# A four-layer attention and feed-forward kernel: turned rows by VectorE and transfers, slot stores on GpSimd's queue, biases inside the opening's products

## The chip, the cores and the metric

The kernel runs on one core of one Trainium2 chip. A core has five engines that run side by side: TensorE (PE, matrix products), VectorE (DVE), ScalarE (ACT), GpSimd (POOL) and SyncE (SP, which here only issues transfers). Each engine works through its own queue of instructions in the order in which they were written, and waits for others by semaphores. Transfers (DMAs) can be issued from SP, ACT and POOL. The metric is the time of one execution on the device in microseconds (us).

## The reference

The computation carries x of shape (4, 256, 256) through four layers; every layer adds an attention over a context of shape (4, 512, 128) and then a feed-forward block. All of it is in float32.

```python
x = x + _L0_xattn_ref(_layernorm(x, axis=-1), ctx_1024, ...)   # 16 heads of 16, head norms, biases
x = x + _L0_ffn_ref(_layernorm(x, axis=-1), ...)               # best 4 of 64 rank-16 maps
x = x + _L1_xattn_ref(_layernorm(x, axis=-1), ctx_1024, ...)   # 16 heads of 128, 8 key heads
x = x + _L1_ffn_ref(_layernorm(x, axis=-1), ...)               # shared expert + best 2 of 8 experts
x = x + _L2_xattn_ref(...); x = x + _L2_ffn_ref(...)           # one of 2 experts per token
x = x + _L3_xattn_ref(...); x = x + _L3_ffn_ref(...)           # best 64 tokens of each batch
```

Layer 0 projects the normalised rows to queries (with bias bq) and the context to keys and values (with biases; the last 16 context tokens have weights and biases of their own), takes the mean out of each head and divides by its deviation, and then attends. Layer 1's block sends every token to two of eight experts.

## The kernel before, in words

The four engines that compute are put under an order written out by hand (`manual_schedule`, line 1033 and later): their instructions stand in their queues as the Python code issues them. SP's queue alone is ordered by the compiler's scheduler, by what is ready.

The matrix products are float32, and the profile shows two records for each. A product needs its operands with the contracted dimension on the partitions, so rows have to be turned. Normalised rows are turned by `layernorm_T` (line 938): four TensorE transposes against an identity into a PSUM bank, then one ScalarE copy to SBUF (line 947). `context_T` (line 906) does the same for the 512 tokens of one batch's context. `turned1` (line 2189) does it for the rows that the first routed block needs, and stores these rows to DRAM (`xd`).

The opening (lines 1037 to 1572). Loads are issued from SP and ACT, among them the rows of norm parameters `prm` (line 1048, from ACT) and three short bias rows `crow` (lines 1061 to 1065, from SP). VectorE takes head means out of the weights and of `crow`. `spread_biases` (line 1165) multiplies `takes`, a small 0/1 matrix, with `crow`, so that every partition holds the biases; ScalarE copies that to `bqk`. `project_q` and `project_k` (lines 1184 and 1200) make the products, and a VectorE addition puts `bqk` to them on the way out of PSUM. The class `Scale` squares, sums, and scales the heads; `transposed` (line 1337) turns them; the first `scores` follow. `warm` (line 1441) issues products that nobody reads, to fill gaps on TensorE.

Attention of layers 1 to 3 (line 1795): 32 units (4 batches of 8 pairs of heads). Every unit makes the next unit's queries, four score products, the exponentials, and four value products. In unit 3 of a batch, the next batch's rows are normalised (`tokens`, line 2039); in unit 5 `layernorm_T` turns them (line 2046); in unit 6 `x_sums` (line 2048, VectorE) reads them, and in unit 7 the first queries of the next batch. In layer 1, `beside1` (line 2248) does the same for the routed block's rows: normalised in unit 4, turned in unit 5, read in unit 6 by `chosen`.

The routed block of layer 1 (lines 2265 to 2622). 20 blocks of 128 slots each belong to one expert. For block j the methods are `gather` (line 2436, an indirect DMA from POOL that brings 128 rows of `xd` into `xg`, four buffers), `turn_in` (two TensorE transposes of `xg`), `rise`, `fall`, `last_rows` (products) and `store` (line 2497: ScalarE scales the result into `yr`, SP's queue writes it to DRAM, `yd`). The loop that orders them is:

```python
for j in range(-1, NBLK + 1):                    # line 2567
    if j + 2 < NBLK:
        if j + 2 >= 4:
            blocks[j + 2].gather()
        if j >= 0:
            blocks[j + 2].weights()
        blocks[j + 2].turn_in()
    ...                                          # rise of j+1, fall of j
        if j % 2 or j == NBLK - 1:               # every second turn: last_rows, then store, of both
```

So blocks go by pairs. In the turn after a pair's stores, the code issues the gather of the block four further on than the pair's first, and TensorE's first work of that turn is to transpose what this gather brings. When all 20 are stored, `Back` (line 2505) gathers the results from `yd`, and the weights of layer 2 are folded (`folding`, line 981; its products `pn` go to the banks "o" and "s").

The routed block of layer 2 ends with a loop over its last blocks (line 3046), in which `backs[n].add()` and the norm of the next layer's first rows stand at i = 6, and `tokens` at i = 7.

Of the kernel before, what the change touches and what calls it, by code (L numbers as in the profile page):

```python
# [17 lines left out]
P = 128  # L18
# [818 lines left out]
def bounded_path(ctx: ExitStack, tc: tile.TileContext, t, out: bass.AP, over):  # L837
# [10 lines left out]
    w0 = first.enter_context(tc.tile_pool(name="w0", bufs=2, side="right"))  # L848
    ring = first.enter_context(ExitStack())
# [104 lines left out]
    def normalised(name):  # L954

        after = layernorm(0, f"{name}_0")
        for b in range(B):
            _, xnT = after
            if b + 1 < B:
                after = layernorm(b + 1, f"{name}_{b + 1}")  # L960
            yield b, xnT
# [19 lines left out]
    def folding(L, m_sb, n_sb):  # L981

        for i in range(4):
            h0 = 4 * i
            if (L, i) not in raws:
                load_raw(L, i)
            wq_t, wk_t, wv_t, wo_t = raws.pop((L, i))
            for g in range(2):
                pm = bank("mm", [P, ND, 2, DC], f"pm_{L}_{i}_{g}")
                for d in range(ND):  # L990
                    for h in range(2):
                        nc.tensor.matmul(  # L992
                            pm[:, d, h, :],
                            lhsT=wq_t[:, 2 * g + h, d * P : (d + 1) * P],
                            rhs=wk_t[:, g, :],
                            start=True,
                            stop=True,
                        )
                h1 = h0 + 2 * g
                nc.scalar.mul(m_sb[:, :, h1 : h1 + 2, :], pm, 1.0 / math.sqrt(P))  # L1000
                m2 = rawp.tile([P, ND, 2, DC], F32, tag="m2", name=f"m2_{L}_{i}_{g}", bufs=1)
                for h in range(2):
                    nc.scalar.activation(
                        m2[:, :, h, :], m_sb[:, :, h1 + h, :], AF.Square,
                        accum_out=msq[:, L - 1, h1 + h : h1 + h + 1],
                    )
                pn = bank("mm" if "ring" in banks else "os"[g], [P, 2, D], f"pn_{L}_{i}_{g}")
                nc.tensor.matmul(  # L1008
                    pn, lhsT=wv_t[:, g, :], rhs=wo_t[:, 2 * g : 2 * g + 2, :], start=True, stop=True
                )  # L1010
                nc.vector.tensor_copy(n_sb[:, h1 : h1 + 2, :], pn)
                yield
# [20 lines left out]
    with tc.manual_schedule(engines={E.PE, E.Activation, E.DVE, E.Pool}):  # L1033
# [13 lines left out]
        for i, n in enumerate(("qn", "kn", "knd")):  # L1047
            nc.scalar.dma_start(prm[:, i], t[f"L0_{n}"].partition_broadcast(P))
# [6 lines left out]
        rows1 = w0.tile([3, D + 3 * P], F32, tag="oT0", name="rows1")  # L1055
# [3 lines left out]

        brow = l0.tile([1, 2, 2 * D], F32, tag="brow", name="brow")  # L1060
# [31 lines left out]
        make_identity(nc, ident)  # L1092
        nc.gpsimd.memset(neghalf, -0.5)

# [3 lines left out]
        nc.gpsimd.memset(takes, 1.0)  # L1098
        for i, base, cm, p in (
            (0, 0, -1, 0), (1, -1, 1, 0), (1, 1, -1, 0), (2, RD - 1 - P, P, -1), (2, 2 * P - RD, -P, 1),  # L1100
        ):
            nc.gpsimd.affine_select(
                out=takes[:, i, :], in_=takes[:, i, :], compare_op=ALU.is_ge, fill=0.0, base=base,
                pattern=[[p, P]], channel_multiplier=cm,
            )
# [78 lines left out]
        def project_q(b):  # L1184
            raw_heads(b)
            pq = bank("mm", [P, NC, D], f"pq0_{b}")
            for c in range(NC):
                for d in range(ND):
                    nc.tensor.matmul(
                        pq[:, c, :],  # L1190
                        lhsT=xnTs[b][:, d, c * P : (c + 1) * P],
                        rhs=wq0[:, d, :],
                        start=(d == 0),
                        stop=(d == ND - 1),
                    )
            return lambda: nc.vector.tensor_tensor(
                qks[b][:, :NC, :], pq, bqk[:, 0:1, :].to_broadcast([P, NC, D]), ALU.add
            )

        def project_k(b, k0):  # L1200
            raw_heads(b)
            pk = bank("mm", [P, 2, D], f"pk{b}_{k0}")
            for k in (k0, k0 + 1):
                last = k == NK - 1
                ck = c_last[:, b % 2, 0, :] if last else cT[:, b, k * P : (k + 1) * P]
                nc.tensor.matmul(pk[:, k - k0, :], lhsT=ck, rhs=wk0[:, 0, :], start=True, stop=not last)
                if last:
                    nc.tensor.matmul(
                        pk[:, k - k0, :], lhsT=c_last[:, b % 2, 1, :], rhs=wk0[:, 1, :], start=False, stop=True
                    )  # L1210
            bias = bqk[:, 1:3, :] if k0 + 2 == NK else bqk[:, 1:2, :].to_broadcast([P, 2, D])
            return lambda: nc.vector.tensor_tensor(qks[b][:, NC + k0 : NC + k0 + 2, :], pk, bias, ALU.add)
# [20 lines left out]
        class Scale:  # L1233


            def __init__(self, b):
                self.src = by_head(qks[b])
                self.dst = pad.rearrange("p c q (h x) -> p c (q h) x", x=HD0)
                self.sq = w0.tile([P, NQK, H0, HD0], F32, tag="hs", name=f"hs{b}", bufs=1)
                self.v, self.r, self.e = (  # L1240
                    small.tile([P, NQK, H0], F32, tag=f"h{i}", name=f"h{i}_{b}", bufs=2) for i in "vre"
                )

            def square(self, on_act, a=0, z=NQK):
                sq, src = self.sq[:, a:z], self.src[:, a:z]
                if on_act:
                    nc.scalar.activation(sq, src, AF.Square)
                else:
                    nc.gpsimd.tensor_tensor(sq, src, src, ALU.mult)
# [25 lines left out]
            def scaled(self, a=0, z=NQK):  # L1275
                nc.vector.tensor_tensor(
                    self.dst[:, a:z], self.src[:, a:z],
                    self.r[:, a:z, :, None].to_broadcast([P, z - a, H0, HD0]), ALU.mult,
                )
# [57 lines left out]
        def transposed(b, c0, wait=False):  # L1337
# [5 lines left out]
            pt = bank("t", [P, 2, 2, P], f"pT{b}_{c0}")  # L1343
# [176 lines left out]
        norm = Norm(0, "a0_0")  # L1520
        last_context(0)
# [5 lines left out]
        centred(by_head(crow), by_head(crow), head_sums(by_head(crow), 3), 3)  # L1527
        wk = by_head(wkv, 2 * HD0)[:, :, :, :HD0]
        centred(by_head(wk0), wk, head_sums(wk))
        for n in range(2):  # L1530
            wv = by_head(wkv, 2 * HD0)[:, n, :, HD0:].rearrange("p (q j o) x -> p o q j x", q=2, o=2)
            for o in range(2):
                nc.gpsimd.tensor_copy(wvo[:, n, o].rearrange("p (q j) x -> p q j x", q=2), wv[:, o])
        columns_of_norms()
        warm(3)
        add_q = project_q(0)
        spread_biases()
        add_q()
        sc0 = Scale(0)
        sc0.square(True, 0, NC)  # L1540
        add_k = [project_k(0, k0) for k0 in range(0, NK, 2)]
        add_k[0]()
        sc0.square(True, NC, NC + 2)
        sc0.sum(0, NC)
        add_k[1]()
        sc0.power(0, NC)
        sc0.square(True, NC + 2, NQK)
        context_T(1)
        sc0.sum(NC, NC + 2)
        ones_of_values()  # L1550
        sc0.root_aside(0, NC)
        last_context(1)
        sc0.sum(NC + 2, NQK)
        sc0.power(NC, NQK)
        kept = []
# [3 lines left out]
        warm(2)  # L1559
        sc0.scaled(0, NC)  # L1560
        second = transposed(0, 0, True)
        warm(4)
        sc0.root(NC, NQK)
        sc0.scaled(NC, NC + 2)
        transposed(0, 2)
        sc0.scaled(NC + 2, NQK)
        second()
        transposed(0, 4)
        warm(2)
# [19 lines left out]
        def between(b, i):  # L1589

            n = b + 1
            if n == 1:
                if i == 0:
                    for k0 in range(0, NK, 2):
# [16 lines left out]
            elif n < B:  # L1611
                if i == 0:
                    context_T(n)
# [17 lines left out]
            if n + 1 < B:  # L1631
                if i == (5 if n == 1 else 6):
# [162 lines left out]
    def attention(L, m_sb, n_sb, first_xnT=None, after=None, at_end=None, chunk=None, within=None):  # L1795
# [13 lines left out]
        with tc.tile_pool(name=f"att{L}", bufs=2) as ap:  # L1809
            xnTs, xns, xxs, norms, qTs, pqs, outs, sums = {}, {}, {}, {}, {}, {}, {}, {}  # L1810
# [223 lines left out]
            for n, (b, hp) in enumerate(units):  # L2034
                if b + 1 < B:
                    if hp == 1:
                        norms[b + 1] = Norm(b + 1, f"a{L}_{b + 1}")
                    elif hp == 3:
                        xns[b + 1] = norms[b + 1].tokens()
# [5 lines left out]
                if b + 1 < B and hp == 5:  # L2045
                    xnTs[b + 1] = layernorm_T(xns[b + 1], f"a{L}_{b + 1}")
# [142 lines left out]
    def turned1(b, xn):  # L2189
        nc.sync.dma_start(xd[b * S : (b + 1) * S, :].rearrange("(c p) d -> p c d", p=P), xn)  # L2190
        xnT1[b] = fx.tile([P, ND, S], F32, tag=f"xnT{b}", name=f"xnT_f1_{b}")
        pt = bank("t", [P, ND, S], f"pxn_f1_{b}")
# [55 lines left out]
    def beside1(b, hp):  # L2248
        if b == 0:
            load_waiting(2)  # L2250
        if b > 0:
            if hp == 3:
                ahead1[b] = Norm(b - 1, f"f1_{b - 1}")
            elif hp == 4:
                ahead1[b] = ahead1[b].tokens()
            elif hp == 5:
                turned1(b - 1, ahead1[b])
# [7 lines left out]
    with tc.manual_schedule(engines={E.PE, E.Activation, E.DVE, E.Pool}):  # L2265
        back = ExitStack()
        backp = back.enter_context(tc.tile_pool(name="back", bufs=4, side="right"))
        with tc.tile_pool(name="f1", bufs=2) as fp:
# [161 lines left out]
            class Block:  # L2430
# [66 lines left out]
                def store(self):  # L2497
# [5 lines left out]
                    nc.sync.dma_start(yd[j * P : (j + 1) * P, :], yr)  # L2503
# [483 lines left out]
    with tc.manual_schedule(engines={E.PE, E.Activation, E.DVE, E.Pool}):  # L2987
# [3 lines left out]
        with tc.tile_pool(name="f2", bufs=2) as fp, tc.tile_pool(name="raw3", bufs=4) as rawp:  # L2991
# [54 lines left out]
            for i in range(5, NBLK2):  # L3046
# [5 lines left out]
                if i + 1 < NBLK2:  # L3052
                    rise2(i + 1)
                    if i + 2 < NBLK2:
                        blocks2[i + 2].weights(fp)
                    blocks2[i + 1].either()
# [7 lines left out]
                if i == 6:  # L3064
                    for n in range(NC):
                        backs[n].add()
                    norm = Norm(0, "a3_0")
                if i == 7:
# [385 lines left out]
```

## Time and profile before

| what | value |
|---|---|
| time, median of 3 runs | 1388.01 us (1386.84 to 1388.09) |
| the profiled execution | 1386.64 us, of which the span from the first to the last instruction is 1384.9 us |
| TensorE busy | 1374.5 us (99%) |
| VectorE busy | 887.1 us (64%) |
| GpSimd busy | 683.9 us (49%) |
| ScalarE busy | 580.2 us (42%) |
| DMA packets | 50849, of them 2544 from GpSimd's queue |
| first scores of layer 0 start at | 21.28 us |
| the 20 routed blocks of layer 1 | about 581.5 to 634 us |

A row of the timeline gives the start in us, the length in us of what is merged in it, the engine, the line, the operation, and in brackets how long the engine sat idle before it and what ended that. A row of the windows gives a stretch's borders and length, then the busy time (and count) of PE, PEld (weight loads), DVE, ACT and POOL, then the granted clock of TensorE, the busy share of the DMA engines and GB/s.

### The profile page before, as it was taken

The page shows a single profiled execution, that of the slowest core. Times are in us where ns is not written, and L with a number is a line of the kernel's source. Part 1 is how long each engine was busy: PE and PEld are TensorE (multiplying, and loading weights), DVE is VectorE, ACT ScalarE, POOL GpSimd, SP SyncE. Part 2 cuts the span into 40 slices and gives each one's busy share as a digit, 9 for nine tenths or more (in the row PEclk, how much of TensorE's full clock was granted, in tenths as well). Part 3 has the DMA queues.
Part 4 walks back from the last instruction along what each step waited for, and adds up shares of the span by engine and source line. Part 5 has one row for each costly group of instructions (what it writes and reads, how often), then busy time and mean ns, then how long its engine had stood idle before and what let it go on. Part 6 is the DMA issues. An engine that isn't in the chain of part 4 may idle for free.

```text
span 1384.9 us, 20011 instructions
## 1 busy us (share of the span) xinstructions
PE 1374.5 (99%) x7277; PEld 908.1 (66%) x7277; DVE 887.1 (64%) x2026; ACT 580.2 (42%) x1148; POOL 683.9 (49%) x829
## 2 busy tenths in 40 slices
PE   9999999999999999999999999999999999999998
PEld 7665676566656667887565666666975656666667
DVE  6667863665666547655666756558656758566676
ACT  5766454433343332356434333333364344333331
POOL 4223333566565445232577654556315675445561
PEclk9999999999999999999999999999999999999999
DMA  5000220300000001172110000000332000000001
GB/s 170 2 1 2 76 77 21 78 17 1 9 0 9 1 9 34 47 238 67 39 54 8 16 1 9 0 0 16 120 117 65 8 4 4 0 1 0 1 0 34
DMA packets 50849, 47.10 MB, mean 34 GB/s; under 512 B 8755, under 2 KB 46868, under 8 KB 50742
## 3 DMA queue, kind: packets, MB, share of 16 engines
q1 hardware_dynamic: 46406, 37.69, 8.9%
q0 software_dynamic: 2544, 6.95, 1.8%
q8 instruction: 60, 0.98, 0.3%
q10 hardware_dynamic: 1792, 1.10, 0.3%
q14 instruction: 47, 0.39, 0.1%
HBM read 38.78 MB, written 6.95 MB: 33 GB/s over the span
## 4 chain that ended last, share of the span: by engine, by line
PE 95%; POOL 2%; DVE 1%; DMA 1%; issue 0%; ACT 0%; ACTq 0%; SPq 0%; POOLq 0%; DVEq 0%
PE ps L1923 23%; PE po L1931 23%; PE paq L1893 6%; PE pao L1893 5%; PE pbq L1893 4%; PE pbo L1893 4%; PE ps L1378 3%; PE po L1388 2%; PE pyf L1512 2%; PE paf L1462 2%; PE pgu L2471 2%; PE psh L2292 2%; PE py L2017 2%; PE pn L1008 1%; PE pb L2876 1%; PE pm L992 1%
## 5 line engine op out<-in xcount | busy, mean ns | idle before, releaser
L1942 POOL TENSOR_TENSOR half<-pT 128x1024 f32<-128x1024 f32 x93 | 218.4, 2349 | 287.1 <-ACT pT L1926 214.8
L1923 PE MATMUL ps<-qT,cT 128*128 128x512 f32 x768 | 345.6, 593 | 0.0
L1931 PE MATMUL po<-pT,c_sb 128*128 128x512 f32 x768 | 345.3, 592 | 0.0
L1926 ACT ACTIVATE pT<-ps,mbias 128x512 f32<-128x512 f32 x384 | 263.8, 687 | 155.3 <-PE ps L1923 140.0
L1931 PEld LDWEIGHTS po<-pT,c_sb 128*128 128x128 f32 x768 | 145.8, 190 | 183.2 <-issue 183.2
L1923 PEld LDWEIGHTS ps<-qT,cT 128*128 128x128 f32 x768 | 138.9, 190 | 138.4 <-issue 136.3
L1935 ACT COPY oT<-po 128x512 f32<-128x512 f32 x96 | 56.2, 586 | 265.2 <-PE po L1931 265.2
L1978 POOL TENSOR_TENSOR oT<-oT,wide 128x512 f32<-128x512 f32 x84 | 106.8, 1292 | 0.0
L1903 DVE TENSOR_TENSOR qT<-qT,paq 128x128 f32<-128x128 f32 x90 | 25.5, 283 | 96.0 <-ACT qT L1902 96.0
L1382 ACT ACTIVATE pT<-ps 128x512 f32<-128x512 f32 x128 | 66.0, 602 | 25.8 <-PE ps L1378 25.6
L1950 DVE TENSOR_TENSOR half<-half 128x512 f32<-128x512 f32 x96 | 71.8, 748 | 2.7 <-POOL half L1940 2.5
L1952 DVE STREAM_TRANSPOSE turned<-half 128x512 f32<-128x512 f32 x96 | 68.3, 711 | 6.3
L1903 DVE TENSOR_TENSOR w<-w,pao 128x128 f32<-128x128 f32 x21 | 6.0, 286 | 103.0 <-ACT w L1902 103.0
L1893 PE MATMUL paq<-xnT_a,m_sb 128*128 128x128 f32 x360 | 71.4, 280 | 0.0
L1893 PE MATMUL paq<-xx,m_x 128*128 128x128 f32 x360 | 69.6, 275 | 0.0
L1893 PEld LDWEIGHTS paq<-xnT_a,m_sb 128*128 128x128 f32 x360 | 57.2, 192 | 16.7 <-issue 8.5
L1956 DVE TENSOR_REDUCE sums<-turned 128x16 f32<-128x512 f32 x96 | 65.9, 686 | 3.3
L1893 PE MATMUL pao<-n_x,ox 128*128 128x128 f32 x336 | 65.0, 275 | 0.0
L1902 ACT COPY qT<-paq 128x128 f32<-128x128 f32 x90 | 23.9, 265 | 94.1 <-PE paq L1893 94.1
L1906 DVE TENSOR_TENSOR qT<-qT,pbq 128x384 f32<-128x384 f32 x90 | 49.9, 554 | 9.7 <-DVE qT L1905 0.5
L1893 PEld LDWEIGHTS paq<-xx,m_x 128*128 128x128 f32 x360 | 54.7, 192 | 0.0
L1977 DVE STREAM_TRANSPOSE wide<-rz 128x512 f32<-128x512 f32 x84 | 54.4, 686 | 0.0
(490 smaller groups left out, 2547.3 us busy)
## 6 DMA issues: line engine op xcount, KB each, us to landing
wq<-in_L_wqT SPq DMA_DIRECT2D x11, 512.0 KB, 4.2
wo<-in_L_wo SPq DMA_DIRECT2D x11, 512.0 KB, 5.1
yd<-yr SPq DMA_DIRECT2D x20, 128.0 KB, 3.6
xd<-xn_f SPq DMA_DIRECT2D x8, 256.0 KB, 2.3
w<-in_F_w SPq DMA_DIRECT2D x4, 512.0 KB, 3.3
wk<-in_L_wkT SPq DMA_DIRECT2D x11, 128.0 KB, 4.0
wv<-in_L_wvT SPq DMA_DIRECT2D x11, 128.0 KB, 4.4
yd<-yb SPq DMA_DIRECT2D x9, 128.0 KB, 2.4
```

The lines of the kernel that those rows point to most:

```text
L1382: nc.scalar.activation(pT[kp][:, j], ps[j], AF.Exp)
L1893: nc.tensor.matmul(p[:, at, :], lhsT=lhsT, rhs=rhs, start=(k == 0 and at == 0), stop=(k == len(of) - 1 and i == which[-1]),)
L1923: nc.tensor.matmul(ps, lhsT=cT[:, b, k * P : (k + 1) * P], rhs=qT, start=True, stop=True)
L1926: nc.scalar.activation(pT[:, k, :], ps, AF.Exp, bias=mbias[:, b, k : k + 1])
L1931: nc.tensor.matmul(po, lhsT=c_sb[:, b, k, :], rhs=pT[:, k], start=(k == 0), stop=(k == NK - 1))
L1935: done["head"] = nc.scalar.copy(raw, po).ins
L1942: nc.gpsimd.tensor_tensor(half, pT[:, 0:2], pT[:, 2:4], ALU.add)
L1950: nc.vector.tensor_tensor(part, half[:, 0], half[:, 1], ALU.add)
L1952: nc.vector.transpose(turned.rearrange("p f i -> p (f i)"), part)
L1956: nc.vector.tensor_reduce(sums[b, hp // 4][:, hp % 4, :], turned, AX.X, ALU.add)
L1977: nc.vector.transpose(wide, rzs[b, hp // 4][:, hp % 4, :, None].to_broadcast([P, NB, 32]))
L1978: eng.tensor_tensor(outs[b, hp], outs[b, hp], wide.rearrange("p f i -> p (f i)"), ALU.mult)
```

## The change

- `layernorm_aside` turns rows without TensorE: two VectorE transposes, each of 32x32 squares within 128x256, and then 16 DMAs of SP's queue, each moving one 32-partition group of squares (4 runs of 32 floats per partition) to its place. It replaces `layernorm_T` in the attention of layers 1 to 3 (issued in unit 3 with the tokens; 3 batches of each layer) and the turning in `turned1` for the first three batches (issued in unit 4). `turned_aside` does the same for the contexts of batches 2 and 3 in layer 0, two and more units before they are read, in place of `context_T`. Rows of layer 0, and the rows at the beginnings of layers, are still turned by TensorE.
- The store of a slot block is issued from `nc.gpsimd` in place of `nc.sync`.
- In the opening the loads of `prm` move from ACT's queue to POOL's. `crow` and `takes` get 128 rows (the unused ones zero, `crow` cleared by GpSimd first), and for batch 0 each of the six 128x256 pieces of q and k gets one further product `takes` x `crow` accumulated into its PSUM bank; `Scale` then reads PSUM directly. The VectorE additions of batch 0 and the early `spread_biases` go; `spread_biases` is issued in the first turn of batch 0's attention, for the later batches. `takes` is built after the first norm. In SP's queue the three loads of `crow` now stand behind the loads of all contexts and all rows of x. Some fillers are added, some removed.
- The folding of layer 2 uses bank "s" (four buffers) for `pn`. In the last loop of layer 2's routed block the `add`s move to i = 7, before `either`, the norm to the end of i = 7, the tokens to i = 8.

```diff
+    def turned_aside(dst, src, name):
+        y = squares([P, 4, 4, 32], f"y_{name}", True)
+        nc.vector.transpose(
+            y.rearrange("p q n s -> p n q s"), src.rearrange("p (n q s) -> p n q s", q=4, s=32)
+        )
+        to = dst.rearrange("p (n i s) -> p i n s", i=4, s=32)
+        for i in range(4):
+            for q in range(4):
+                nc.sync.dma_start(to[32 * q : 32 * q + 32, i], y[32 * i : 32 * i + 32, q])
+
+    def layernorm_aside(xn, name, xnT, soon=False):
+        y = squares([P, 4, ND, NC, 32], f"y_{name}", soon)
+        for c in range(NC):
+            nc.vector.transpose(
+                y[:, :, :, c].rearrange("p q d s -> p d q s"), xn[:, c, :].rearrange("p (d q s) -> p d q s", d=ND, s=32)
+            )
+        to = xnT.rearrange("p d (c i s) -> p i d c s", c=NC, s=32)
+        for i in range(4):
+            for q in range(4):
+                nc.sync.dma_start(to[32 * q : 32 * q + 32, i], y[32 * i : 32 * i + 32, q])
+        return xnT
...
-                pn = bank("mm" if "ring" in banks else "os"[g], [P, 2, D], f"pn_{L}_{i}_{g}")
+                pn = bank("mm" if "ring" in banks else "s" if L == 2 else "os"[g], [P, 2, D], f"pn_{L}_{i}_{g}")
...
-            nc.scalar.dma_start(prm[:, i], t[f"L0_{n}"].partition_broadcast(P))
...
-        rows1 = w0.tile([3, D + 3 * P], F32, tag="oT0", name="rows1")
+        rows1 = w0.tile([P, D + 3 * P], F32, tag="oT0", name="rows1")
...
+        nc.gpsimd.memset(crow, 0.0)
...
+            nc.gpsimd.dma_start(prm[:, i], t[f"L0_{n}"].partition_broadcast(P))
...
+                if b == 0:
+                    nc.tensor.matmul(pq[:, c, :], lhsT=takes[:, 0, :], rhs=crow[:, 0, :], start=False, stop=True)
+            if b == 0:
+                return pq
...
+                if b == 0:
+                    nc.tensor.matmul(
+                        pk[:, k - k0, :], lhsT=takes[:, 1 + int(last), :], rhs=crow[:, 0, :], start=False, stop=True
+                    )
+            if b == 0:
+                return pk
...
-        spread_biases()
-        add_q()
...
+        pieces = {0: project_q(0)}
+        for k0 in range(0, NK, 2):
+            pieces[NC + k0] = project_k(0, k0)
+        sc0 = Scale(0, pieces)
...
                 if i == 0:
+                    spread_biases()
                     for k0 in range(0, NK, 2):
                         project_k(n, k0)()
...
-                    context_T(n)
...
+                if i == 2:
+                    turned_aside(cT[:, n + 1, :], c_sb[:, n + 1].rearrange("p k c -> p (k c)"), f"c{n + 1}")
...
                     elif hp == 3:
-                        xns[b + 1] = norms[b + 1].tokens()
+                        name = f"a{L}_{b + 1}"
+                        xnTs[b + 1] = layernorm_aside(norms[b + 1].tokens(), name, rows_tile(name))
...
-                if b + 1 < B and hp == 5:
-                    xnTs[b + 1] = layernorm_T(xns[b + 1], f"a{L}_{b + 1}")
...
             elif hp == 4:
-                ahead1[b] = ahead1[b].tokens()
-            elif hp == 5:
-                turned1(b - 1, ahead1[b])
+                turned1(b - 1, ahead1[b].tokens(), True)
...
-                    nc.sync.dma_start(yd[j * P : (j + 1) * P, :], yr)
+                    nc.gpsimd.dma_start(yd[j * P : (j + 1) * P, :], yr)
...
+                    else:
+                        for n in range(NC):
+                            backs[n].add()
...
-                if i == 6:
-                    for n in range(NC):
-                        backs[n].add()
+                if i == 7:
                     norm = Norm(0, "a3_0")
-                if i == 7:
+                if i == 8:
                     xn = norm.tokens()
```

## The prediction

> **What bounds the kernel now.** I read the page's busy times and chain first, then the waits of TensorE, then windows by stage, then the timelines of the two stages that the change reorders.
>
> ```profile
> PE 1374.5 (99%) x7277; PEld 908.1 (66%) x7277; DVE 887.1 (64%) x2026; ACT 580.2 (42%) x1148; POOL 683.9 (49%) x829
> PE 95%; POOL 2%; DVE 1%; DMA 1%; issue 0%; ACT 0%; ACTq 0%; SPq 0%; POOLq 0%; DVEq 0%
> ...
> PE pyb L2902 <- DVE yb L2906: 1.2, 1, 1.2
> PE pn L1008 <- DVE n_sb L1011: 0.3, 1, 0.3
> ```
>
> TensorE is never free: its waits add up to some 6 us, of which 1.2 and 0.3 are places that the change touches. So a transpose taken from TensorE is a gain of its full time, and a stall put before TensorE is a loss of its full time. Only the opening (scores start at 21.28) is a chain through all engines.
>
> In the routed blocks TensorE is dense too. The rows of one pair of blocks, engine by engine (timelines; the last from the DMA list, with the median us from issue to landing):
>
> ```profile
> 580.42 0.95 POOL L2438 DMA_INDIRECT xg<-xd,who  x1 [1.41 <-PE pxg L2446]
> ...
> 587.22 0.38 PE L2495 MATMUL pyr<-wd,gR 48*128 x1
> 587.53 0.44 PE L2446 MATMUL pxg<-ident,xg 128*128 128x128 f32 x2
> 592.28 0.44 PE L2446 MATMUL pxg<-ident,xg 128*128 128x128 f32 x2
> ...
> 587.63 0.84 ACT L2500 ACTIVATE yr<-pyr,wslot 128x256 f32<-128x256 f32 x2 [0.46 <-PE pyr L2495]
> 588.13 1.04 SPq L2503 DMA_DIRECT2D yd<-yr  x2
> ...
> 578.07 0.95 POOL L2438 DMA_INDIRECT xg<-xd,who  x1 [0.30 <-issue]
> 638.06 0.94 POOL L2512 DMA_INDIRECT yg<-yd,where  x1 [23.16 <-DMA yd<-yr]
> ...
> xg<-xd,who POOLq DMA_INDIRECT x25, 3.2
> ```
>
> A pair takes 587.53 to 592.28, 4.75 us. Block 4's gather was issued at 580.42, as soon as its buffer was free, 7.1 us before TensorE turned its rows (587.53). This lead exists because POOL's queue holds nothing but gathers here.
>
> **Part 1, the slots' stores on POOL's queue.** The loop issues the two stores of a pair, and in the next turn the gather for that turn's `turn_in`. In the built order of the changed kernel POOL's queue reads: gathers 0 to 3, stores 0 and 1, gathers 4 and 5, stores 2 and 3, gathers 6 and 7, and so on; and TensorE's first instruction after `last_rows` of blocks 0 and 1 is the transpose of block 4, with a wait for its gather. So the gather is now queued behind stores that wait for ScalarE, which waits for TensorE's last rows: a loop through four engines, once for each pair. With the end of `last_rows` (587.60) as zero:
>
> - ScalarE's first `yr` is ready and the first store can issue at 0.55 (SP's row: 588.13).
> - Two stores on POOL. No row shows a plain store there. Lower bound: the 0.34 of SP's issue plus the 0.30 gap, 0.65 each. Nearest row: an indirect DMA of equally many rows on the same queue, 0.95 + 0.30 = 1.25. I take 1.25; upper bound 2.
> - The gather issues at 0.55 + 2.5 = 3.05 and lands 3.2 later (the row; 2.7 to 3.7 in this stage), at 6.25; TensorE goes on at about 6.35 in place of -0.07: a stall of 6.4 us.
>
> The second gather follows 1.25 after the first, and TensorE needs it 2.05 later (587.53 to 589.57), so it costs nothing. Stalls come before blocks 4, 6, ... 18: eight, 8 x 6.4 = 51.2 us. Nothing else can run on TensorE meanwhile, since it too works in order.
>
> Then the clock. The granted clock (the third figure from the right of a window's row) reads 1.00 from the start, so by this column a restarted TensorE is at full speed, and the sum stays 51.2. But the fillers at the start were slow:
>
> ```profile
> 1.52 4.21 PE L1445 MATMUL pwarm<-ident 128*128 128x128 f32 x18 [1.52 <-POOL ident masks.py:199]
> 5.53 1.06 PE L910 MATMUL pcT<-ident,c_sb 128*128 128x128 f32 x4
> ...
> 18.65 1.06 PE L1445 MATMUL pwarm<-ident 128*128 128x128 f32 x8
> 19.68 1.23 PE L1346 MATMUL pT<-ident,pad 128*128 128x128 f32 x8
> ...
> 2.00:4.00 2.00, 2.00 (x11) 2.00 (x11) 0.27 (x2) 0.00 (x0) 2.00 (x9) 1.00 0.62 202
> ```
>
> 18 records in 4.01 us are 223 ns each, later 8 in 1.03 are 129. [...] No stall of this length is in the trace, so the fall is not shown; I take it, as the start shows the slow state: 8 x 8.6 = 68.8 us. Loads of layer 2's weights, tied to the stores' ScalarE copies, move with the blocks.
>
> **Part 2, turning without TensorE.** Removed: nine `layernorm_T` in attention, three in `turned1`, two `context_T`; each 4 transposes, 0.44 us from start to start (587.53's two cost 0.22 to 0.27; `pxn` at 1020.00 to 1020.43 is 0.43). 14 x 0.44 = -6.2 us, and as many ScalarE copies of 0.59 that nobody waited for. Added: two VectorE transposes, by the 128x512 row of 0.71 some 0.76 the two; VectorE is busy 64% and in unit 3 needs its sums a unit (8.43 us) later: nothing. 16 DMAs on SP, at 0.35 to 0.58 an issue (rows of line 894) 7 us, the last landing 2 to 4 later: some 11 us. Cover: tokens in unit 3, `x_sums` in unit 6, 25 us; for `turned1` end of unit 4 to end of unit 6, 17 us; the contexts 15 us. SP's loads that wait for the head of unit 2 stand among them, but that is over by then. If a batch were late it would hold VectorE at `x_sums` and then the queries; I leave 0 to +5 for it.
>
> **Part 3, the opening.** What the biases now wait for:
>
> ```profile
> 4.93 0.52 SPq L1063 DMA_DIRECT2D rows<-in_L_bdca  x1
> 7.93 0.41 DVE L1152 TENSOR_REDUCE hm<-rows 3x16 f32<-3x256 f32 x1 [0.27 <-DMA rows<-in_L_bdca]
> ...
> 21.28 1.25 PE L1378 MATMUL ps<-qT,kT 32*128 32x256 f32 x16
> ```
>
> The last bias load issued at 4.93 and landed 3.0 later. In the new order it is SP's thirteenth load, behind x of batch 3, and each of SP's loads waits for an earlier landing; that x waits for the second half of `wkv`, which landed at 7.1 (SP's next load, held for it, went out at 7.11) and now shares the engines with two more contexts and rows (to 7.9). Three issues of 0.4 to 0.65 later the last bias load goes out at about 9.4 and lands at 12.3. VectorE's two steps (0.41 each): 13.15. First bias product 13.2; TensorE's queue is stuck behind it, with the q and k products of 0.45 each: q ready at 15.0 (in place of 13.5), k at 16.8 and 19.05. Then square 0.63, sum 0.86, scaling of q 0.68, the root 0.7, scaling of k 0.65, transposes 0.45, columns 0.8: scores at about 24.1, +2.8 us. If the biases were early, the three additions saved would make it 20.8 (-0.5); if TensorE fell cold in its 3 us wait, +5.5. `prm` on POOL holds the first `rstd` by up to 0.7, inside this wait. `spread_biases` moves into dense attention: three products, +1.4.
>
> **Small ones.** Fold bank -0.3; the adds behind `z` free line 2902's wait, -1.2.
>
> **Sum** on the profiled execution: 1386.6 + 68.8 - 6.2 + 2.8 + 1.4 - 1.5 = 1451.9; its median run is 1.4 above it, so 1453 us.
>
> **The rivals.**
> - The stalls come, the clock stays: 1453 - 8 x 2.2 = 1435. For it: the column of 1.00. Against: the fillers.
> [...]
> - The other side: stores do not hold the gathers, because POOL passes over a waiting DMA. Then 1388.0 - 6.2 + 2.8 + 1.4 - 1.5 = 1384.5, just faster. It decides where a gather goes out before the pair's stores have. Against: the row at 638.06 sat 23 us on one wait, and the queues of SP and ACT stood behind waiting loads in the opening. From a stall of 0.4 us on (3.5 / 8) the change is slower.
> [...]
>
> **How the numbers follow.** Full stalls with the fall of the clock 0.60 (1440 to 1470); stalls with a full clock 0.18; short stalls 0.13; heavier 0.05; no stalls 0.04. The range leaves out the last two and the ends of the others: 1422 to 1472. Slower by over 0.2% (2.8 us, about what a measurement of this kernel can tell) 0.96, faster 0.03, same 0.01.
>
> **What would show it.** Right: the stretch of the routed blocks grows from 52 to some 120 us; TensorE sits idle eight times before `pxg`, 6 us each, released by the DMA of `xg`; POOL's rows alternate two stores and two gathers, stores waiting for `yr`; records of `pgu` after a stall near twice their length; no `pxn` in units 5; no wait of VectorE for turned rows; first scores near 24. Wrong: gathers that still run 7 us ahead, or stalls of another length (then the POOL row of a store and the gather's landing say which term).

## The result, and the profile after

The changed kernel takes 1461.39 us (median of 5 runs, 1460.76 to 1462.91) against 1387.64 for the kernel before (5 runs): a ratio of 1.0534, 95% interval 1.0519 to 1.0549, so 5.3% slower. 1453 was predicted, in a range of 1422 to 1472. The place and the kind of the loss were as forecast. The length of the opening and the landing times of the gathers were not, and two small costs came up that the sum did not have.

The page of the changed kernel, its busy times, the chain of work that ended last, and two of its costliest groups (busy us, mean ns of one, idle time before it and what ended that):

```profile
PE 1390.6 (95%) x7241; PEld 922.3 (63%) x7241; DVE 896.7 (61%) x2049; ACT 573.6 (39%) x1134; POOL 699.2 (48%) x853
...
PE 89%; issue 5%; POOL 3%; DMA 1%; DVE 1%; ACT 0%; SPq 0%; POOLq 0%; DVEq 0%
...
L2486 PE MATMUL pxg<-ident,xg 128*128 128x128 f32 x40 | 10.9, 366 | 54.0 <-DMA xg<-xd,who 54.0
...
L2543 POOL DMA_DIRECT2D yd<-yr x20 | 11.5, 578 | 96.0 <-ACT yr L2540 96.0
```

TensorE was at 99% of the span and is at 95%. Its busy time rose by 16 us although 56 transposes left it: the same products take longer. The list of its waits (engine, line, what it waited for; total, times, longest) has two that are new:

```profile
PE pxg L2486 <- DMA xg<-xd,who: 54.0, 8, 8.4
PE pq L1222 <- DVE rows L1181: 5.6, 1, 5.6
```

The wait of `pyb` for `yb` (1.2) and that of `pn` (0.3) are gone, and none for turned rows has come. The routed blocks, all engines (timeline):

```profile
594.79 0.84 ACT L2540 ACTIVATE yr<-pyr,wslot 128x256 f32<-128x256 f32 x2 [0.45 <-PE pyr L2535]
595.57 1.17 POOL L2543 DMA_DIRECT2D yd<-yr  x2 [11.54 <-ACT yr L2540]
595.66 0.37 SPq L998 DMA_DIRECT2D n_sb<-in_L_wqT  x1
...
597.04 1.01 POOL L2478 DMA_INDIRECT xg<-xd,who  x1 [0.30 <-issue]
597.16 0.51 SPq L998 DMA_DIRECT2D n_sb<-in_L_wo  x1
...
603.09 0.66 PE L2486 MATMUL pxg<-ident,xg 128*128 128x128 f32 x2 [8.33 <-DMA xg<-xd,who]
603.54 2.77 PE L2511 MATMUL pgu<-xgT,we 128*128 128x128 f32 x12
607.38 2.09 PE L2511 MATMUL pgu<-xgT,we 128*128 128x128 f32 x12
...
611.35 1.15 POOL L2543 DMA_DIRECT2D yd<-yr  x2 [12.01 <-ACT yr L2540]
612.80 1.00 POOL L2478 DMA_INDIRECT xg<-xd,who  x1 [0.30 <-issue]
```

This is the forecast loop: `last_rows`, `yr`, two stores, and only then the gather for which TensorE stands still. The eight stalls are 8.33, 5.10, 8.42, 5.12, 8.34, 5.12, 8.30 and 5.26 us. The long ones are those at which SP sends out layer 2's weights (595.66 to 597.67). After a stall the 12 records of `pgu` take 2.77 us, and those of the next block up to 2.15; undisturbed they take 1.49. The windows of the opening and of the stage's first half (length; busy us, with records, of PE, PEld, DVE, ACT and POOL; granted clock, DMA share, GB/s) in the changed kernel:

```profile
0.00:21.00 21.00, 13.37 (x63) 11.49 (x64) 8.40 (x24) 3.77 (x7) 8.81 (x29) 0.84 0.70 199
...
578.00:640.00 62.00, 38.00 (x200) 32.49 (x200) 16.31 (x48) 12.77 (x38) 14.58 (x18) 0.78 0.24 78
```

The same stretches in the kernel before:

```profile
0.00:21.00 21.00, 18.67 (x103) 16.50 (x104) 14.74 (x38) 8.97 (x19) 11.35 (x48) 1.00 0.63 191
...
578.00:640.00 62.00, 61.79 (x433) 51.33 (x433) 29.36 (x79) 31.64 (x95) 17.84 (x19) 1.00 0.55 168
```

In the blocks TensorE now works 38 of 62 us, at a mean granted clock of 0.78, where it worked 61.8 at 1.00. The opening is at 0.84 in place of 1.00. So the column does show falls of the clock, which it had not shown in the kernel before. The opening in rows, and two windows of it:

```profile
11.32 0.57 SPq L1085 DMA_DIRECT2D rows<-in_L_bdca  x1
...
14.01 0.41 DVE L1176 TENSOR_REDUCE hm<-rows 3x16 f32<-3x256 f32 x1 [3.63 <-DMA rows<-in_L_bdca]
...
14.96 1.19 PE L1222 MATMUL pq<-rows 128*128 128x256 f32 x2 [5.57 <-DVE rows L1181]
...
18.52 0.60 ACT L1287 ACTIVATE hs<-pq 128x512 f32<-128x512 f32 x1 [10.31 <-PE pq L1222]
...
24.81 1.50 PE L1385 MATMUL pT<-ident 128*128 128x128 f32 x12
...
29.32 1.15 PE L1420 MATMUL ps<-qT,kT 32*128 32x256 f32 x16
...
14.00:16.00 2.00, 1.04 (x3) 0.89 (x4) 1.67 (x7) 0.00 (x0) 0.00 (x0) 0.50 0.26 69
16.00:18.00 2.00, 2.00 (x6) 1.63 (x5) 0.00 (x0) 0.00 (x0) 0.00 (x0) 0.50 0.40 80
```

The bias rows land at 14.0, the first products after TensorE's wait run at a granted clock of 0.50, q is ready at 18.5, and the first scores start at 29.32 in place of 21.28: +8.0.

Booked by places that both profiled executions have (start of the record, before and after):

| place | before | after | shift | since the last |
|---|---|---|---|---|
| first scores of the first layer | 21.3 | 29.3 | +8.0 | opening +8.0 |
| first scores of the second layer | 224.3 | 232.2 | +7.9 | +0.9 behind the first scores (the size is that of the run of the opening alone, below), two contexts -0.9 |
| lists of the routed stage, `plist` | 568.4 | 573.9 | +5.5 | six turnings, -2.4 |
| transposes of block 0 | 579.8 | 586.9 | +7.1 | +1.6: not in the prediction |
| last `pxg` of the blocks | 623.4 | 701.3 | +77.9 | stalls and clock, +70.8 |
| lists of the two-expert stage | 958.3 | 1035.2 | +76.9 | three turnings, -1.0 |
| last `pyb` of that stage | 1018.0 | 1093.6 | +75.6 | order of the adds, -1.3 |
| last `pxg` of the last stage | 1368.5 | 1442.7 | +74.2 | three turnings, -1.4 |
| end of the span | 1384.9 | 1461.2 | +76.3 | +2.1: not in the prediction |

### The profile page after: what moved, and what is told of

Read it like the earlier page. It is cut to its first block, busy times and chain, and to the rows that moved or that the text cites. A ratio compares the mean times of both kernels' runs of the same rounds, so it can differ in the third digit from the quotient of the medians.

```text
span 1461.2 us, 20280 instructions
## 1 busy us (share of the span) xinstructions
PE 1390.6 (95%) x7241; PEld 922.3 (63%) x7241; DVE 896.7 (61%) x2049; ACT 573.6 (39%) x1134; POOL 699.2 (48%) x853
## 4 chain that ended last, share of the span: by engine, by line
PE 89%; issue 5%; POOL 3%; DMA 1%; DVE 1%; ACT 0%; SPq 0%; POOLq 0%; DVEq 0%
PE ps L1963 22%; PE po L1971 22%; PE paq L1933 6%; PE pao L1933 5%; PE pbq L1933 4%; PE pbo L1933 4%; PE ps L1420 3%; PE po L1430 2%; PE pyf L1554 2%; PE paf L1504 2%; PE psh L2332 1%; PE py L2057 1%; PE pm L1014 1%; PE pn L1030 1%; PE pb L2916 1%
## 5 line engine op out<-in xcount | busy, mean ns | idle before, releaser
L1933 PEld LDWEIGHTS paq<-xnT_a,m_sb 128*128 128x128 f32 x360 | 57.5, 192 | 18.2 <-issue 9.2
L2522 DVE TENSOR_TENSOR gT<-sg,pgu 128x128 f32<-128x128 f32 x20 | 5.8, 288 | 92.3 <-ACT sg L2517 92.3
L2486 PE MATMUL pxg<-ident,xg 128*128 128x128 f32 x40 | 10.9, 366 | 54.0 <-DMA xg<-xd,who 54.0
L2543 POOL DMA_DIRECT2D yd<-yr x20 | 11.5, 578 | 96.0 <-ACT yr L2540 96.0
```

Source lines behind the costliest of these rows:

```text
L1933: nc.tensor.matmul(p[:, at, :], lhsT=lhsT, rhs=rhs, start=(k == 0 and at == 0), stop=(k == len(of) - 1 and i == which[-1]),)
```

## The experiments

None of these kernels leaves a part of the computation out. Each ratio is against the kernel before as it ran on the same chip at the same time (1387.8 or 1388.7 us there), so the ratio is the safer number; a plain difference from 1461.4 us can be off by about 1 us.

**The parts alone.** First the changed kernel with its one line of the store undone:

```diff
-                    nc.gpsimd.dma_start(yd[j * P : (j + 1) * P, :], yr)
+                    nc.sync.dma_start(yd[j * P : (j + 1) * P, :], yr)
```

> The changed kernel with one line undone: the slots' stores on SP again. Theory (the gathers queue behind the stores): the eight stalls of 54.0 us go, and with them the 16 us that the products after them lose to the clock; what is left beside the kernel before is the opening (scores 8.0 us later), the products of spread_biases (+1.4), the turning (-6.2) and the small edits (-1.5): 1387.6 + 1.7 = 1389, and a stretch of routed blocks of 52 us. Rival (the rest of the change takes part in the loss, as by its small transfers): over 1400.

Measured: 1389.74 us (12 runs), ratio 1.0013 (1.0004 to 1.0021). Of the 74 us, 72 hang on this line; what is left of the change is 2 us of loss. The opposite, that line alone in the kernel before:

> The kernel before with that one line changed: the slots' stores on GpSimd and nothing else. Theory: all of the 54.0 us of stalls and 16 us of clock: 1387.6 + 70 = 1458, granted clock near 0.78 in the routed blocks. Rival A (the stalls come, the clock falls for another reason, as the colder opening): 1387.6 + 54 = 1442. Rival B (the stores do not hold the gathers): 1387 to 1389.

Measured: 1459.94 us (4 runs), ratio 1.0520 (1.0502 to 1.0539). Its wait:

```profile
PE pxg L2446 <- DMA xg<-xd,who: 54.3, 8, 8.5
```

The same 54 us, and the rest of the change takes no part in it. Between the profiled spans lie 72.8 us (1384.9 and 1457.7): 54.3 of stalls, and 18.5 that rival A would not have (1.9 of them are at the end of the program, see the last section). The third and fourth runs put the turning alone and the opening alone into the kernel before:

```diff
# the turning: unit 3 of attention, and likewise turned1 and the contexts
-                        xns[b + 1] = norms[b + 1].tokens()
+                        xnTs[b + 1] = layernorm_aside(norms[b + 1].tokens(), name, rows_tile(name))
-                if b + 1 < B and hp == 5:
-                    xnTs[b + 1] = layernorm_T(xns[b + 1], f"a{L}_{b + 1}")
# the opening: the edits of the diff from prm to transposed(0, 4), and spread_biases in unit 0
```

> The kernel before with only the turning: 14 sets of transposes replaced by VectorE transposes and 16 small transfers each. Theory: 14 x 0.44 us of TensorE saved and nothing late: 1387.6 - 6.2 = 1381.4. Rival (a batch of transfers is late and holds VectorE and TensorE): -1 to +5, 1386 to 1393.

Measured: 1381.78 us (6 runs, 1379.66 to 1383.66), ratio 0.9950 (0.9936 to 0.9964): -6 us, as reckoned.

> The kernel before with only the opening: biases by full-height products, their rows loaded after the contexts, prm on GpSimd, fillers inside the transposes' bank, spread_biases in attention. Theory (as the changed kernel's trace has it: scores at 29.3 in place of 21.3): 1387.6 + 8.0 + 1.4 = 1397. Rival (the prediction's chain of +2.8, the rest of the 8.0 being taken back by cover later in the stage): 1387.6 + 2.8 + 1.4 = 1392.

Measured: 1396.6 us (5 runs), ratio 1.0058 (1.0045 to 1.0072), +8.8: nothing of the late scores (8.2 us in this run) is taken back later. The parts add up: 72 (store) + 8.8 - 6.0 - 1.5 (small edits: the predicted size, not run by themselves) = 73.3, for 73.8 measured.

**Is it GpSimd's queue, or the place in it?** The stores stay on GpSimd, and the next pair's gathers are written ahead of a pair's stores:

```diff
-                    if j + 2 >= 4:
-                        blocks[j + 2].gather()
...
                         for one in pair:
                             one.last_rows()
+                        for n in (j + 3, j + 4):
+                            if 4 <= n < NBLK:
+                                blocks[n].gather()
                         for one in pair:
                             one.store()
```

> The changed kernel, its slots' stores still on GpSimd, but the two gathers of the next turns written ahead of a pair's stores (their buffers were freed by the transposes before). Theory (only the place behind the waiting store matters): no wait for xg, 1461.4 - 54.0 - 16 = 1391, as with the stores on SP. Rival (GpSimd's queue is a slow way for stores, or stores and gathers hold each other in the DMA engines whatever their order): a part of the stalls stays, over 1405.

Measured: 1415.9 us (4 runs), ratio 1.0196 (1.0180 to 1.0212). By the number this is the rival's case (over 1405): 46 us came back, and four stalls stayed. What held them shows in the wait and in the timeline of GpSimd's queue and of TensorE:

```profile
PE pxg L2486 <- DMA xg<-xd,who: 16.0, 4, 5.0
```

```profile
595.51 1.17 POOL L2543 DMA_DIRECT2D yd<-yr  x2 [5.51 <-ACT yr L2540]
596.98 1.01 POOL L2478 DMA_INDIRECT xg<-xd,who  x1 [0.30 <-issue]
...
603.46 0.66 PE L2486 MATMUL pxg<-ident,xg 128*128 128x128 f32 x2 [4.01 <-DMA xg<-xd,who]
```

The edit moves the gathers ahead of one pair's stores and leaves them behind those of the pair before it. Block 6's gather goes out at 596.98, and TensorE is ready for it at 599.45 (603.46 less 4.01): a lead of 2.5 us, against a landing of 6.5 beside layer 2's loads. So the theory had to be said more exactly: what counts is the lead of the gather on the transposes, and a gather cannot go out before the store ahead of it can. If that is so, one pair more of lead must do it:

```diff
+                if j % 2:
+                    for n in (j + 5, j + 6):
+                        if n < NBLK:
+                            blocks[n].gather()
                 if 0 <= j < NBLK:
                     blocks[j].fall()
# the gather at the head of the turn goes, as in the run before
```

> The changed kernel, stores on GpSimd, with each pair's gathers written two pairs ahead, behind the stores of the pair two before their own (four buffers are enough: the transposes of block j + 2 are done). In the run with gathers one pair ahead, a gather issued 1.47 us behind a store of the pair before had 2.4 us of lead on its transposes. Theory (only this lead counts): 2.4 + 4.75 = 7.1 us, as in the kernel before, against landings of 2.8 to 6.2, no stall: 1389.7 to 1392. Rival (stores on GpSimd's queue hold the gathers in another way too): stalls stay beside layer 2's loads, over 1400.

Measured: 1390.86 us (10 runs), ratio 1.0017 (1.0008 to 1.0027), beside 1.0013 with the stores on SP. No wait for `xg` is left. The stage has the window of the kernel before again (61.97 us busy, clock 1.00), with all 20 stores on GpSimd:

```profile
578.00:640.00 62.00, 61.97 (x432) 51.97 (x432) 31.75 (x92) 27.42 (x84) 31.56 (x38) 1.00 0.52 166
```

So GpSimd's queue is as good for the stores as SP's, but for the end of the program (last section). The order in it made the loss.

**The clock.** Products that nobody reads fill TensorE's wait:

```diff
                     pt = bank("to"[self.j % 2], [P, ND, P], f"pxg{self.j}")
+                    fill = 20 if self.j >= 4 and self.j % 2 == 0 else 0
+                    for _ in range(fill):
+                        nc.tensor.matmul(pt[:, 0, :], lhsT=ident, rhs=ident, start=True, stop=True)
```

> The changed kernel with 20 products of ident with ident (some 5.2 us) on TensorE ahead of the transposes of blocks 4, 6, ... 18, so that it works while it waits for a gather; nothing is computed with them. Theory (after the stalls the clock is down and costs 1.5 us after a stall of 5.1 and 2.6 after one of 8.4): the gathers land as before, the products after them run at full speed: 1461.4 - 16 = 1445, granted clock near 1.00 there. Rival (the products after a stall are slow for another reason, as late weights or a late copy): 1461 to 1463.

Measured: 1453.38 us (4 runs), ratio 1.0466 (1.0450 to 1.0482): -8 us (-9 by the ratios) of the 16. The fillers last 4.73 us, which covers the short stalls and not the long ones, and the timeline splits just so:

```profile
603.32 0.69 PE L2489 MATMUL pxg<-ident,xg 128*128 128x128 f32 x2 [3.70 <-DMA xg<-xd,who]
603.80 2.77 PE L2514 MATMUL pgu<-xgT,we 128*128 128x128 f32 x12
607.64 2.29 PE L2514 MATMUL pgu<-xgT,we 128*128 128x128 f32 x12
...
616.10 0.44 PE L2489 MATMUL pxg<-ident,xg 128*128 128x128 f32 x2 [0.45 <-DMA xg<-xd,who]
616.38 1.49 PE L2514 MATMUL pgu<-xgT,we 128*128 128x128 f32 x12
618.36 1.49 PE L2514 MATMUL pgu<-xgT,we 128*128 128x128 f32 x12
```

After 0.45 us of idleness the products take their undisturbed 1.49 us, though the gather came no earlier than without fillers; after 3.70 they are as slow as after 8.3. That rules out late weights and late copies: idleness of TensorE is what slows them. The expected gain of 16 had assumed that any shortening of a wait would do.

**The long landings.** Layer 2's loads held for a later copy:

```diff
-                    nc.scalar.copy(self.xgT, pt)
+                    done["turned"] = nc.scalar.copy(self.xgT, pt).ins
...
-                if j in (5, 9, 13):
-                    load_raw(2, j // 4, done["slots"])
+                if j in (6, 10, 14):
+                    load_raw(2, j // 4, done["turned"])
# and the first set likewise, at j == 2 in place of 1
```

> The changed kernel with the four sets of loads for layer 2's weights (1.25 MB each) held for the copy of xgT after a stall instead of for the copy of yr before it. Theory (they take the DMA engines from the stores and gathers of every second pair, whose landing is 6.1 us and not 2.8): all eight stalls become 5.1 us, so 4 x 3.3 = 13 us less of stalls and 4 x 1.1 less lost to the clock, 1461.4 - 17.5 = 1444. Rival (the long landings come from the list of rows or from the page of the gather): 1461, long stalls where they were.

Measured: 1450.86 us (4 runs), ratio 1.0457 (1.0440 to 1.0474): -10.5 us.

```profile
PE pxg L2486 <- DMA xg<-xd,who: 42.7, 8, 5.9
```

The stalls are now 5.1 to 5.9 us all eight, 11.3 less, so the long landings were the loads'. The second half of the expectation fell: the records of `pgu` sum to 42.5 us, against 42.7 in the changed kernel. The `pgu` of the second block after a stall takes 1.49 us three times and 1.55 to 2.31 five times, all after stalls of 5.1 to 5.9. In the changed kernel and with the line alone it took 1.49 after each stall of that length and 2.05 to 2.21 after each of 8.2 to 8.5. So the length of the stall alone does not set the price of a fall; what does stays open.

**The opening.** The changed kernel, stores on SP, with the rows' loads on ScalarE's queue:

```diff
-        nc.sync.dma_start(crow[0:1, 0, :], t["L0_bq"].partition_broadcast(1))
+        nc.scalar.dma_start(crow[0:1, 0, :], t["L0_bq"].partition_broadcast(1))
# the other two rows likewise
```

> The changed kernel with its slots' stores on SP (1389.7 measured) and the three bias rows loaded from ScalarE's queue behind wkv, and so ahead of the contexts. Theory (the late rows are the larger part of the opening's loss): the bias product is then held by VectorE's centring of wk, which ends at 10.4, plus 0.8 for the rows: 11.2 in place of 15.0, -3.8; TensorE waits 1.8 us and stays warm, -0.7; scores near 24.9: 1389.7 - 4.5 = 1385.2. Rival (the longer chain of products, sums and fillers binds anyway): 0 to -1.5, 1388 to 1390.

Measured: 1390.84 us (11 runs), ratio 1.0018 (1.0009 to 1.0027): no gain. But the run does not test the theory, since the rows were no earlier, nor the estimate of -0.7 for a TensorE that waits 1.8 us, since it waited 5.02:

```profile
8.29 0.49 ACTq L1083 DMA_DIRECT2D rows<-in_L_bq  x1
...
11.57 0.53 ACTq L1085 DMA_DIRECT2D rows<-in_L_bdca  x1
12.14 0.59 ACT L912 COPY cT<-pcT 128x512 f32<-128x512 f32 x1 [8.50 <-DMA c_sb<-in_ctx]
...
13.27 2.08 PE L1214 MATMUL pq<-wq,xnT_a 128*128 128x256 f32 x4 [5.02 <-ACT xnT_a L948]
```

The loads waited on this queue too (the trace does not say for what), and ScalarE's copies stood behind them, so that the wait only moved to `xnT`. The next run does without the full height: there is no memset of 128 rows that the loads follow, and SP sends the rows third to fifth, as in the kernel before. VectorE takes their means ahead of those of `wk`. The stores are on SP here too.

```diff
-        rows1 = w0.tile([P, D + 3 * P], F32, tag="oT0", name="rows1")
+        rows1 = w0.tile([3, D + 3 * P], F32, tag="oT0", name="rows1")
-        nc.gpsimd.memset(crow, 0.0)
# and centred(three, ...) ahead of centred(by_head(wk0), ...)
```

> The changed kernel with its slots' stores on SP (1389.7), and the products of the biases over 3 rows in place of 128: no memset of the rows, so that their loads stand on SP where the kernel before has them (landed at 7.9 there), and VectorE centres them ahead of wk as there. Theory (the full height made the rows late, and that is the opening's loss but for 1.5 us of fillers): bias product at about 9 and without a stall, q ready at 11.2 in place of 18.5, so scores near 22 in place of 29.4, 1389.7 - 7.3 = 1382.4. Rival (the longer chain behind the products binds in its place): scores at 25 or later, 1385 or more.

Measured: 1383.57 us (5 runs), ratio 0.9963 (0.9949 to 0.9977), 0.5% less than the same with full-height products (1.0013).

```profile
2.85 0.59 SPq L1084 DMA_DIRECT2D rows<-in_L_bdca  x1
...
9.53 0.69 PE L1221 MATMUL pq<-rows 3*128 3x256 f32 x2
...
11.94 0.60 ACT L1286 ACTIVATE hs<-pq 128x512 f32<-128x512 f32 x1 [3.53 <-PE pq L1221]
12.46 0.69 PE L1241 MATMUL pk<-rows 3*128 3x256 f32 x2
13.09 0.70 PE L1235 MATMUL pk<-wk,cT 128*128 128x256 f32 x2
...
24.44 1.15 PE L1419 MATMUL ps<-qT,kT 32*128 32x256 f32 x16
```

The rows' side of the theory holds: no stall, q ready at 11.9 (11.2 expected). The scores start at 24.4 and not at 22, so both cases were half right. From q to the scores it now takes 12.5 us, 10.8 in the changed kernel, 7.7 in the kernel before (13.55 to 21.28). Products of 3 and of 128 rows in turn start every 0.63 us (12.46, 13.09), where those of full height start every 0.43 in the changed kernel (18.32, 18.75), at a granted clock of 1.00 (18.3 to 21.0 us) in the latter; the next run has the same 0.63, and its granted clock is 1.000 on the mean of the whole run. That is what the full height buys, 0.2 us a step over the nine steps of k. Then the fillers:

```diff
-        second = transposed(0, 0, True, 6)
+        second = transposed(0, 0, True, 0)
# and 0 in place of 5 and 1 in the two other calls
```

> The same without the 12 fillers in the bank of the transposes. Theory (24 records stand ahead of the transposes of q and k, which have their operands): another 1.5 us, scores near 20.5, 1381. Rival (they stand in time that is free, or keep the clock up): no gain, 1382.4 or more.

Measured: 1383.82 us (5 runs), ratio 0.9966 (0.9952 to 0.9979): no gain that shows. In the trace the scores start at 23.7 in place of 24.4, though the first q product came 0.5 later in this run; so about 1.2 us are won where they stood, which the times do not resolve. The expected 20.5 was not reached.

**A version that beats both**: the turning and the small edits, the opening and the stores as before.

> The kernel before with the turning, the fold's bank and the order of the adds in the expert stage, its own opening, stores on SP. Theory: turning measured at -6.0, small edits -1.5: 1387.8 - 7.5 = 1380.3. Rival (the list stage, where the turning's profiled run shows a granted clock of 0.50 for 5 us, takes the gain back): 1383 to 1385.

Measured: 1378.51 us (5 runs, 1378.33 to 1381.80), ratio 0.9936 (0.9922 to 0.9949): 0.6% faster than the kernel before. By the ratios it is 1.9 us below the turning alone; the small edits had been reckoned at 1.5. The rival did not come up in the profiled execution, where the list stage has a clock of 1.00.

## Why the prediction was right, and where it was not

**Part 1, right; its terms differ and cancel.** The step "the gather is now queued behind stores that wait for ScalarE" is shown by the two runs of the line alone and by the one with the far gathers. The first store issues 0.8 us after `last_rows` (0.55 predicted). The two stores take 1.47 to the gather's issue, not 2.5: a plain store costs 0.58 on GpSimd, and half of the 1.47 is 0.74, nearer to my lower bound of 0.65 than to the indirect row's 1.25 that I took. The landing term was mis-sized the other way: from its issue to TensorE's start it was 2.84 us beside the pair's own stores and 6.05 beside layer 2's loads too, where I took 3.2. The prediction had said that these loads "move with the blocks" and priced that at nothing; it is the same moment, the copy `yr`, that lets loads, stores and (now) gathers go. The stall was 6.75 on the mean, with 6.4 predicted: that the sum came so close, with two of its terms wrong in opposite directions, is luck.

**The clock, right in size, by a term that no run shows.** Per stall 2.1 us (72.7 between the profiled spans of the changed kernel and of the one with its stores on SP, less 54.0 of stalls, less 1.9 at the end of the program, over 8); the sum has 2.2 (8.6 less 6.4). That term was an estimate of mine, and no run shows what it was made of. The runs show this in its place: after the changed kernel's stalls of 5.10 to 8.42 the first `pgu` took 2.77 us each time, and after the waits of 3.47 to 5.0 with the gathers ahead and of 3.70 to 4.52 with the fillers, 8 in all, 2.6 to 2.8, while after four waits of 0.37 to 0.51 it took 1.49. No wait for `xg` in these runs lies between 0.51 and 3.47 us, so what one of that length costs is not shown. The rival "the clock stays" is out.

**Part 2, right.** -6.2 predicted; -6.0 measured alone, and -5.7 as the four shares in the table. VectorE's two transposes took 0.76 as forecast. SP's 16 issues took 10 to 12 us in place of 7, each landing in 1.8, inside the 25 us of cover. VectorE never waited for turned rows.

**Part 3, wrong in size: +8.0 for +2.8.** Three steps fell short. The last bias row landed at 14.0, not 12.3. From the first bias product to q I reckoned 1.8 us at full clock; after 5.6 us of idleness, at a granted clock of 0.50, it took 3.5. That is the case "if TensorE fell cold", which I had named beside the sum (as +5.5, an estimate without a trace behind it) and left out of it. And from q to the scores I took 9.1 us, the old chain with the new products; it took 10.8. My list of steps left out the 24 filler records in front of the transposes; with products of 3 rows, taking them out won about 1.2 us, and at full height that was not tried. Three times some 1.7 make up the 5.2 that were missing. The products of `spread_biases` held TensorE for 1.4 us as predicted (30.39 to 31.79), but the layer behind the first scores became only 0.9 longer in the run of the opening alone; where the other 0.5 came back was not traced.

**Small edits, right**: -1.3 in the expert stage for -1.2.

**Not in the sum**: 1.6 us in the list stage and 2.1 at the program's end, both in the last section. The prediction's 1451.9 for the profiled execution misses 76.3 us of shift by 11.0: 5.2 opening, 2.0 blocks, 2.1 end, 1.6 lists, and 0.1 of the rest. The opening by itself lay outside what I had allowed for it (-0.5 to +5.5); the total stayed in its range because the store's line is 95% of it (72.7 of 76.3).

## What to carry over

Before a DMA is moved to another queue, write down what stands behind it there, and from when on that was free to go. The cost is the lead that it loses, once for each turn of the loop, and no word in the diff touches the gather that pays it. Loads may stand behind a waiting store only if they still go out early enough, that is, if their lead on their reader stays longer than their landing: with 2.5 us of lead against a landing of 6.5 TensorE stood still for 4.0, and with 7.2 in the run with the far gathers (596.84 to 604.07) it did not wait. Take that landing at the moment at which other loads go out too: here it was 6 us in place of 3. If TensorE must wait for a DMA, count the slow products after it as well: here, after stalls of 5.1 to 8.4 us, they cost nearly a third as much again (16.8 on 54.0 us).

## What the runs showed beside this

**A clock of one half where no wait shows.** In the profiled run of the turning alone the lists' 32 products of 40 columns stand among other products, without a wait that the trace shows before or behind them. They are followed by a granted clock of one half (windows of that run):

```profile
560.00:565.00 5.00, 5.00 (x31) 4.51 (x30) 4.72 (x19) 1.15 (x3) 0.00 (x0) 1.00 0.00 0
565.00:570.00 5.00, 4.97 (x36) 4.69 (x35) 3.88 (x21) 0.00 (x0) 0.00 (x0) 0.84 0.01 5
570.00:575.00 5.00, 5.00 (x13) 3.92 (x12) 1.71 (x9) 0.00 (x0) 3.24 (x4) 0.50 0.18 52
```

The same stretch of the kernel before:

```profile
568.40:573.40 5.00, 4.97 (x39) 4.64 (x39) 4.37 (x22) 0.00 (x0) 0.00 (x0) 1.00 0.01 3
573.40:578.40 5.00, 5.00 (x25) 4.17 (x24) 2.53 (x9) 0.38 (x1) 3.81 (x4) 1.00 0.19 52
```

TensorE counts as busy all the time in both. From the lists to block 0's transposes it takes 14.7 us in the one and 11.4 in the other, so 3.3 us of the turning's 6 were lost again in this execution. The changed kernel has it too (0.90 and 0.76 in the same two stretches, the 1.6 us of the table); the run with the far gathers and the fastest version have not (1.00). The instructions there are the same, and the cause stays open. Times and clocks of single runs, in which the mean granted clock is on record, go together: of the six runs of the turning alone, the two at 0.999 took 1379.7 us and the two at 0.997 took 1383.0 and 1383.7; of the five of the fastest version, the three at 0.999 took 1378.3 to 1378.5 and the one at 0.996 took 1381.8. So differences of a few us between kernels contain this too. Whether it is the list stage in each of them is not shown.

**The end of the program.** From the last `pxg` product to the end of the span it takes 16.4 to 16.9 us in the eight kernels whose slot stores are on SP, and 18.2 to 18.5 in the six that have them on GpSimd, some 750 us after the last of these stores. The last instructions are the same. The difference lies behind the last row that the trace has: from there to the end it is 4.2 us in the kernel before and 6.3 in the changed one. Its cause stays open.
